# SS2D scan stage: VectorE's and GpSimd's products and scans held in the written order, and TensorE's other stages held behind the copy of dt * x

## The chip, the cores and the metric

The kernel runs on one core of a Trainium2 chip. The metric is the device time of one execution in microseconds. Engine names in profile lines: PE is TensorE's matmul, PEld its weight load, DVE is VectorE, ACT is ScalarE, POOL is GpSimd, SP is SyncE, which issues the DMAs.

## What is computed

The reference is a sequence of four vision layers on 8 images of 56 x 56 positions and 128 channels. Layers 0, 2 and 3 are deformable convolutions; layer 1 is a VMamba block (SS2D). Only layer 1 is touched. Cut to what matters:

```python
xb = silu(depthwise3x3(split(layer_norm(x) @ in_proj)) + conv_b)   # 256 channels
xs = [xb rowwise, xb columnwise, both reversed]                     # K = 4 directions
dts, B, C = split(x_proj[k] @ xs[k])                                # 8, 16 and 16 rows
dt = softplus(dt_projs[k] @ dts + bias)
h[d, n] = h[d, n] * exp(dt[d] * A[d, n]) + (dt[d] * xs[d]) * B[n]   # scan along 3136 positions
y[d] = sum over n of h[d, n] * C[n]                                 # 16 states n
out = x + out_proj(layer_norm(sum of directions + D * xs) * silu(z)); out += mlp(layer_norm(out))
```

## The kernel before

The kernel is written in a tile framework. It records instructions in the written order, but a scheduler then places them on each engine by priority and by its own model of the durations, and adds the semaphores. The order on an engine can therefore differ from the written one. `issue_after(ins)` is the way to bind it: every instruction recorded in that block on the engine of `ins` is placed after `ins`. It adds an ordering edge for the scheduler and not a wait.

Class `Vss` is layer 1. Its method `scans` runs over 128 steps (8 images, 4 directions, 4 chunks of 784 positions) and in each over 32 units. A unit is one instruction's worth of states: 32 channels (`TC`) by 4 states (`TS`) on the 128 partitions. Eight channel groups `cg` have four units `sg` = 0 to 3 each. One unit goes through these instructions (lines of the kernel before):

- `fetch_dt` and `fetch_row` (SP's DMAs) bring dt, dt * x, B and C, spread over the partitions.
- `spread`, L1297, once for each `cg`: TensorE copies dt * x into PSUM as `dtu` (one buffer of two banks, two matmuls with the identity). It is written three units ahead of unit 0 of its group, right after product 2 of the group before.
- `decay`, L1303: ScalarE writes dA = exp(dt * A) to PSUM (two buffers), one unit ahead.
- `inputs`: the product u = (dt * x) * B. For `sg` 0 to 2 VectorE makes it from `dtu` (L1313, two buffers `u`), written one unit ahead. For `sg` 3 GpSimd makes it from SBUF (L1309, one buffer `up`), written two units ahead.
- the scan, L1406: VectorE writes `h` (three buffers); its last column goes to `st` on ScalarE (L1409).
- `hc` = h * C, L1411: GpSimd (six buffers).
- `add_sums`, L1335: TensorE sums `hc` over the states into `acc`, two units at a time, written three units later. It stands already in an `issue_after` block behind the last spread.
- `open_sums` (L1327) starts `acc` (one buffer) for each 8 units, and `close_sums` (L1346) copies it out on ScalarE.

The same engines carry other work between the units. `prepare` makes the next step's rows: projections on TensorE (L1208, L1221), softplus on ScalarE, one sum and one product on GpSimd (L1228, L1230). `input_stage` is the next image's norm, the conv as nine matmuls for each tile (L1069) and the gate (L1076); `output_stage` is the norm, the output projection and the MLP of finished rows (L1130, L1152, L1170, L1181, and the transposes at L1047). They are generators that the unit loop steps: `prepare` at even units, the other two at odd units and at every fourth. All their matmuls share one PSUM buffer, `misc`, so each waits until ScalarE or VectorE has read the one before.

Of the kernel before, what the change touches and what calls it, by code (L numbers as in the profile page):

```python
# [946 lines left out]
class Vss:  # L947
# [4 lines left out]
    def __init__(self, net, images, src, dst):  # L952
        self.net, self.tc, self.nc, self.d = net, net.tc, net.nc, net.d
        self.images, self.src, self.dst = images, src, dst

    def run(self):
        tc = self.tc
        with ExitStack() as ctx:
            enter = ctx.enter_context
            self.cp = enter(tc.tile_pool(name="v_const", bufs=1))  # L960
            self.img = enter(tc.tile_pool(name="v_img", bufs=1))
            self.prep = enter(tc.tile_pool(name="v_prep", bufs=1))
            self.work = enter(tc.tile_pool(name="v_work", bufs=2))
            self.bg = enter(tc.tile_pool(name="v_bg", bufs=1))
            self.dram = enter(tc.tile_pool(name="v_dram", bufs=2, space=DRAM))
            self.pmisc = enter(tc.tile_pool(name="v_misc", bufs=1, space=PSUM))
            self.pdtu = enter(tc.tile_pool(name="v_pdtu", bufs=1, space=PSUM))
            self.pda = enter(tc.tile_pool(name="v_pda", bufs=2, space=PSUM))
            self.pacc = enter(tc.tile_pool(name="v_pacc", bufs=1, space=PSUM))
            self.weights()  # L970
            self.scans()
# [41 lines left out]

    def misc(self):
        return self.pmisc.tile([128, 512], F32, name="misc", tag="misc")

# [25 lines left out]
    def transpose(self, ps, srcs):  # L1044
        n = srcs[0].shape[0]
        for i, s in enumerate(srcs):
            self.nc.tensor.transpose(ps[:, n * i : n * (i + 1)], s, self.net.ident[:n, :n])  # L1047

    def input_stage(self, i):
        nc, w, n, T = self.nc, self.w, LC // self.NT, self.NT
        both = self.gates[i] = self.dram.tile([128, 2 * NCH, L], F32, name="gate", tag="gate")
        xn = {}

        def slab(c):
            if 0 <= c < NLC and c not in xn:
                xn[c] = self.bg.tile([128, RPC + 2, WP], F32, name="xn", tag="xn", bufs=3)
                nc.gpsimd.memset(xn[c], 0.0)
            return xn.get(c)  # L1060

        def conv(c):

            pre = self.bg.tile([128, 2 * NCH, LC], F32, name="pre", tag="pre")
            for ch in range(NCH):
                ps = self.misc()
                out = ps[:, :LC].rearrange("p (h w) -> p h w", w=W)
                for tap in range(9):
                    nc.tensor.matmul(out, lhsT=w["tap"][:, tap, 128 * ch : 128 * (ch + 1)], rhs=xn[c][:, tap // 3 : tap // 3 + RPC, tap % 3 : tap % 3 + W], start=tap == 0, stop=tap == 8)  # L1069
                    if tap % 3 == 2 and tap < 8:  # L1070
                        yield
                nc.scalar.activation(pre[:, ch, :], ps[:, :LC], AF.Identity, bias=w["conv_b"][:, ch : ch + 1])
                yield
            for ch in range(NCH):
                ps = self.misc()
                nc.tensor.matmul(ps[:, :LC].rearrange("p (h w) -> p h w", w=W), lhsT=w["in"][:, DI + 128 * ch : DI + 128 * (ch + 1)], rhs=xn[c][:, 1 : RPC + 1, 1 : W + 1], start=True, stop=True)  # L1076
                nc.scalar.copy(pre[:, NCH + ch, :], ps[:, :LC])
                yield
            last = nc.scalar.activation(pre, pre, AF.Silu)
            with self.tc.issue_after(last.ins):  # L1080
                nc.scalar.preload_act_table_set(EXP_LN)
            yield
            nc.sync.dma_start(out=both[:, :, LC * c : LC * (c + 1)], in_=pre)
            yield

        for c in range(NLC):
            xt = self.bg.tile([128, T, C], F32, name="xt", tag="xt", bufs=2)
            nc.sync.dma_start(out=xt[:n], in_=self.rows_of(self.src[i], c, n))
            yield
            yield  # L1090
            srcs = [xt[:n, t, :] for t in range(T)]
            rs = self.stats(srcs)
            yield
            z = self.bg.tile([128, T, C], F32, name="z", tag="z", padded_shape=[128, T, DI])
            self.normalize(z, srcs, rs)
            yield
            ps = self.misc()
            self.transpose(ps, [z[:n, t, :] for t in range(T)])
            rows = ps[:, :LC].rearrange("p (h w) -> p h w", w=W)
            for to, a, b, at in ((c, 0, RPC, 1), (c - 1, 0, 1, RPC + 1), (c + 1, RPC - 1, RPC, 0)):  # L1100
                s = slab(to)
                if s is not None:
                    nc.scalar.activation(s[:, at : at + b - a, 1 : W + 1], rows[:, a:b], AF.Identity, bias=w["n1b"], scale=w["n1w"])  # L1103
            yield
            if c:
                yield from conv(c - 1)
        yield from conv(NLC - 1)
# [8 lines left out]
    def output_stage(self, i, c):  # L1116
# [8 lines left out]
        for t0 in range(0, T, 2):  # L1125
            ps = self.misc()
            for t in range(2):
                at = n * (t0 + t)
                for ch in range(NCH):
                    nc.tensor.transpose(ps[:n, DI * t + 128 * ch : DI * t + 128 * (ch + 1)], y[:, ch, at : at + n], self.net.ident)  # L1130
            yield
            yield
            srcs = [ps[:n, DI * t : DI * (t + 1)] for t in range(2)]
            rs = self.stats(srcs)
            yield
            self.normalize(z[:, t0 : t0 + 2], srcs, rs)
            yield
# [11 lines left out]
        po = self.misc()  # L1149
        for t in range(T):  # L1150
            for ch in range(NCH):
                nc.tensor.matmul(po[:n, 128 * t : 128 * (t + 1)], lhsT=gT[:, ch, n * t : n * (t + 1)], rhs=w["out"][:, ch, :], start=ch == 0, stop=ch == NCH - 1)  # L1152
        yield
        yield
        nc.vector.tensor_add(xt[:n], xt[:n], po[:n].rearrange("p (t c) -> p t c", c=128))
# [11 lines left out]
        pre = self.bg.tile([128, NF, m], F32, name="pre", tag="pre", padded_shape=[128, NF, LC])  # L1167
        for f in range(NF):
            ps = self.misc()
            nc.tensor.matmul(ps[:, :m], lhsT=w["fc1"][:, 128 * f : 128 * (f + 1)], rhs=xT, start=True, stop=True)  # L1170
            nc.scalar.activation(pre[:, f, :], ps[:, :m], AF.Identity, bias=w["fc1_b"][:, f : f + 1])
            yield
        last = nc.scalar.activation(pre, pre, AF.Gelu_apprx_tanh)
# [1 line left out]
            nc.scalar.preload_act_table_set(EXP_LN)  # L1175
        yield
        po = self.misc()
        self.net.bias_row(po, n, w["fc2_b"], T)
        for t in range(T):
            for f in range(NF):  # L1180
                nc.tensor.matmul(po[:n, 128 * t : 128 * (t + 1)], lhsT=pre[:, f, n * t : n * (t + 1)], rhs=w["fc2"][:, f, :], start=False, stop=t == T - 1 and f == NF - 1)  # L1181
            if t % 2:
                yield
        nc.vector.tensor_add(xt[:n], xt[:n], po[:n].rearrange("p (t c) -> p t c", c=128))
# [13 lines left out]
    def prepare(self, s, k, c):  # L1198
# [6 lines left out]
        for b in range(2):  # L1205
            ps = self.misc()
            for ch in range(NCH):
                nc.tensor.matmul(ps[:XD, :SH].rearrange("p (a b) -> p a b", b=W), lhsT=w["xproj"][:, ch, k, :], rhs=xs[:, ch, SR // 2 * b : SR // 2 * (b + 1)], start=ch == 0, stop=ch == NCH - 1)  # L1208
            yield
            nc.scalar.copy(dbl[:, SH * b : SH * (b + 1)], ps[:XD, :SH])  # L1210
        nc.sync.dma_start(out=s["rows"].rearrange("n (x e) -> (n x) e", x=2), in_=dbl[RANK:])
# [1 line left out]
        for h in range(NCH):  # L1213
# [4 lines left out]
            for b in range(2):  # L1218
                at = slice(SH * b, SH * (b + 1))
                ps = self.misc()  # L1220
                nc.tensor.matmul(ps[:, :SH], lhsT=w["dt"][:, k, 128 * h : 128 * (h + 1)], rhs=dbl[:RANK, at], start=True, stop=True)  # L1221
                nc.scalar.activation(sp[:, at], ps[:, :SH], AF.Abs, bias=bias)
                nc.scalar.activation(dd[:, 0, at], ps[:, :SH], AF.Relu, bias=bias)
                yield
# [32 lines left out]
    def scans(self):  # L1257
# [34 lines left out]
        def spread(at, t):  # L1292
# [2 lines left out]
            ps = s["dtu", cg] = self.pdtu.tile([128, 2, 512], F32, name="dtu", tag="dtu")  # L1295
            for b in range(2):
                last = nc.tensor.matmul(ps[:, b, :SH], lhsT=self.net.ident, rhs=s["dt", cg][:, 1, SH * b : SH * (b + 1)], start=True, stop=True)  # L1297
            self.last_spread = last.ins

        def decay(at, t):  # L1300
            (i, k, c), s, (cg, sg) = steps[at], state[at], order[t]
# [3 lines left out]
        def inputs(at, t):  # L1305
            s, (cg, sg) = state[at], order[t]
            if on_pool(t):
                u = self.work.tile([128, SC], F32, name="up", tag="up", bufs=1)
                nc.gpsimd.tensor_mul(u, s["dt", cg][:, 1], s["b", sg])  # L1309
            else:  # L1310
                u = self.work.tile([128, SC], F32, name="u", tag="u", bufs=2)
                halves = [v.rearrange("p (x e) -> p x e", x=2) for v in (u, s["b", sg])]
                nc.vector.tensor_mul(halves[0], s["dtu", cg][:, :, :SH], halves[1])  # L1313
            s["u", t] = u

        def place(t):
# [11 lines left out]

        def add_sums(at, group):
            acc = state[at]["acc"]  # L1330
            with self.tc.issue_after(self.last_spread):
                for (cg, sg), hc in group:
                    for b in range(2):
                        r = 64 * b + TC * (cg % 2)
# [27 lines left out]
        for now, (at, t) in enumerate(units):  # L1362
# [40 lines left out]
            hh = self.work.tile([128, SC], F32, name="h", tag="h", bufs=3)  # L1403
            step = 1 if forward else -1
            u, dA = s.pop(("u", t)), s.pop(("dA", t))
            nc.vector.tensor_tensor_scan(hh[:, ::step], dA[:, :SC][:, ::step], u[:, ::step], st[:, t : t + 1], ALU.mult, ALU.add)  # L1406
            if c != (NSC - 1 if forward else 0):
                last = SC - 1 if forward else 0
                nc.scalar.copy(st[:, t : t + 1], hh[:, last : last + 1])  # L1409
            hc = self.work.tile([128, SC], F32, name="hc", tag="hc", bufs=6)  # L1410
            nc.gpsimd.tensor_mul(hc, hh, s["c", sg])  # L1411
            group.append((order[t], hc))
            if t % 2:
                late.append((now + 3, add_sums, (at, group)))
# [86 lines left out]
```

## Time and profile before

| | |
|---|---|
| time, median of 3 runs | 18769.62 us (18749.45 to 18785.21) |
| the profiled execution | 18768.71 us, span 18767.1 us |
| granted TensorE clock over the span | 0.804 |
| busy share of the span | PE 76%, PEld 37%, DVE 81%, ACT 60%, POOL 62% |
| the scans, first to last (L1406) | 2460.6 to 13885.8 us |
| scan, L1406 | 4096 instructions, 1837 ns (with u) and 1832 ns (with up) |
| product u, L1313 | 3072 instructions, 956 ns |
| product up, L1309 | 1024 instructions, 1860 ns |
| product hc, L1411 | 4096 instructions, 1870 ns |
| copy of dt * x, L1297 | 4096 matmul records, 643 ns |
| one tap of the conv, L1069 | 2016 matmul records, 576 ns |

A float32 matmul of the program shows as two records. In a row of instructions, the columns after the bar are busy time, mean length of one in ns, and the engine's idle time just before them with what ended it. A line of waits names who waited, for whom, the total in us, how often, and the longest one.

### The profile page before, as it was taken

The page shows a single profiled execution, that of the slowest core. Times are in us where ns is not written, and L with a number is a line of the kernel's source. Part 1 is how long each engine was busy: PE and PEld are TensorE (multiplying, and loading weights), DVE is VectorE, ACT ScalarE, POOL GpSimd, SP SyncE. Part 2 cuts the span into 40 slices and gives each one's busy share as a digit, 9 for nine tenths or more (in the row PEclk, how much of TensorE's full clock was granted, in tenths as well). Part 3 has the DMA queues.
Part 4 walks back from the last instruction along what each step waited for, and adds up shares of the span by engine and source line. Part 5 has one row for each costly group of instructions (what it writes and reads, how often), then busy time and mean ns, then how long its engine had stood idle before and what let it go on. Part 6 is the DMA issues. An engine that isn't in the chain of part 4 may idle for free. (4 is left out here: it accounts for less than half of the span.)

```text
span 18767.1 us, 237758 instructions
## 1 busy us (share of the span) xinstructions
PE 14211.3 (76%) x79747; PEld 6897.5 (37%) x79747; DVE 15283.9 (81%) x18794; ACT 11183.2 (60%) x21344; POOL 11721.8 (62%) x6462
## 2 busy tenths in 40 slices
PE   6888787678678678678778778777666888577777
PEld 4555422222222222222222222222134666455555
DVE  7777369988988988988988998899967777677776
ACT  4666555566566566566566566666554666455555
POOL 1211079988998988998998998999951121111111
PEclk6777788889889889888889888888876777677767
DMA  8888544444444444344443343444326888578777
GB/s 240 223 221 219 140 146 165 157 167 154 141 144 140 144 146 140 140 149 140 142 149 138 139 153 138 142 147 140 139 97 180 215 214 211 154 207 212 206 213 179
DMA packets 1324266, 3112.23 MB, mean 166 GB/s; under 512 B 84800, under 2 KB 876372, under 8 KB 1255196
## 3 DMA queue, kind: packets, MB, share of 16 engines
q1 hardware_dynamic: 1323020, 3096.79, 54.2%
q8 instruction: 639, 10.47, 0.2%
q14 instruction: 607, 4.97, 0.1%
HBM read 2400.54 MB, written 872.17 MB: 174 GB/s over the span
## 5 line engine op out<-in xcount | busy, mean ns | idle before, releaser
L1411 POOL TENSOR_TENSOR hc<-h,c 128x784 f32<-128x784 f32 x4096 | 7539.9, 1870 | 772.6 <-DVE h L1406 541.5
L1406 DVE TENSOR_TENSOR_SCAN h<-dA,st,u 128x784 f32<-128x784 f32 x3072 | 5567.9, 1837 | 327.3 <-ACT dA L1303 188.4
L1303 ACT ACTIVATE dA<-dt,v_A 128x784 f32<-128x784 f32 x4096 | 3743.1, 915 | 714.3 <-DVE h L1406 713.3
L1313 DVE TENSOR_TENSOR u<-dtu,b 128x784 f32<-128x784 f32 x3072 | 2871.5, 956 | 559.1 <-PE dtu L1297 554.5
L1335 PE MATMUL acc<-hc,v_sum 128*32 128x392 f32 x16384 | 3212.8, 551 | 102.8 <-POOL hc L1411 102.1
L1297 PE MATMUL dtu<-dt,ident 128*128 128x392 f32 x4096 | 2108.6, 643 | 1501.1 <-issue 1100.7
L769 PE MATMUL pt<-ident,sw 112*128 112x112 f32 (+8 forms) x11648 | 1912.5, 302 | 495.2 <-DMA sw<-skew 489.0
L736 POOL MEMSET win<- 128x1820 f32 (+2 forms) x384 | 631.5, 1648 | 2512.1 <-DMA skew<-win 1972.1
L1406 DVE TENSOR_TENSOR_SCAN h<-dA,st,up 128x784 f32<-128x784 f32 x1024 | 1876.1, 1832 | 232.1 <-POOL hc L1411 171.1
L771 ACT COPY st<-pt 128x448 f32<-128x448 f32 (+6 forms) x2912 | 1230.7, 444 | 1348.7 <-PE pt L769 1300.9
L1309 POOL TENSOR_TENSOR up<-dt,b 128x784 f32<-128x784 f32 x1024 | 1904.6, 1860 | 135.1 <-DVE h L1406 124.0
L1409 ACT COPY st<-h 128x1 f32<-128x1 f32 x3072 | 581.4, 189 | 2163.6 <-DVE h L1406 2154.8
L1297 PEld LDWEIGHTS dtu<-dt,ident 128*128 128x128 f32 x4096 | 863.4, 235 | 2555.1 <-issue 1676.0
L733 POOL TENSOR_TENSOR ay<-hat,om 112x756 f32<-112x756 f32 (+2 forms) x192 | 441.2, 2298 | 2141.6 <-ACT hat L729 1891.7
L769 PEld LDWEIGHTS pt<-ident,sw 112*128 112x128 f32 (+8 forms) x11648 | 1339.5, 171 | 1079.6 <-issue 721.0
L1335 PEld LDWEIGHTS acc<-hc,v_sum 128*32 128x32 f32 x16384 | 766.9, 117 | 2478.2 <-issue 1657.8
L745 DVE TENSOR_TENSOR win<-win,patch 112x252 f32 (+2 forms) x3456 | 1569.6, 464 | 51.6 <-DVE bn_st L847 13.7
L742 DVE TENSOR_TENSOR patch<-ay,hat 112x756 f32<-112x756 f32 (+2 forms) x1152 | 1221.9, 1074 | 437.7 <-POOL ay L733 437.4
L780 PE MATMUL yps<-st,xw 120*32 120x48 f32 (+8 forms) x23296 | 1222.2, 296 | 230.5 <-ACT st L771 184.2
L1069 PE MATMUL misc<-xn,v_tap 128*128 128x448 f32 x2016 | 871.1, 576 | 94.2 <-ACT xn L1103 60.0
L822 PE MATMUL ps<-xT,w_fc 128*128 128x448 f32 (+1 forms) x1536 | 790.9, 649 | 111.5 <-ACT xT L817 72.3
L1346 ACT COPY y<-acc 64x392 f32<-64x392 f32 x768 | 576.1, 750 | 409.8 <-PE acc L1335 401.3
(162 smaller groups left out, 19421.5 us busy)
## 6 DMA issues: line engine op xcount, KB each, us to landing
dt<-dds SPq DMA_DIRECT2D x1024, 784.0 KB
sw<-skew SPq DMA_DIRECT2D x224, 1050.0 KB
sw<-skew SPq DMA_DIRECT2D x224, 896.0 KB
b<-rows SPq DMA_DIRECT2D x512, 392.0 KB
c<-rows SPq DMA_DIRECT2D x512, 392.0 KB
dds<-dd SPq DMA_DIRECT2D x256, 784.0 KB
sw<-skew SPq DMA_DIRECT2D x224, 784.0 KB
skew<-win SPq DMA_DIRECT2D x128, 964.7 KB
```

Of the source, the lines that this page charges most:

```text
L742: nc.vector.tensor_mul(patch[:n], bcast(a, 3, KX), bcast(b, 2, KY))
L745: self.last_add = nc.vector.tensor_add(to, to, patch[:n, NCB * p : NCB * (p + 1)]).ins
L769: last = nc.tensor.transpose(ps[:KP, n * g : n * (g + 1)], sw[t0:t1, g, KP * j : KP * (j + 1)], self.net.ident[t0:t1, t0:t1])
L771: nc.scalar.copy(st[:KP, : G * n], ps[:KP, : G * n])
L780: self.nc.tensor.matmul(yps[CG * g : CG * (g + 1), t0:t1], lhsT=xw[:KP, j, CG * g : CG * (g + 1)], rhs=st[:KP, n * g : n * (g + 1)], start ...
L1297: last = nc.tensor.matmul(ps[:, b, :SH], lhsT=self.net.ident, rhs=s["dt", cg][:, 1, SH * b : SH * (b + 1)], start=True, stop=True)
L1303: nc.scalar.activation(da[:, :SC], s["dt", cg][:, 0], AF.Exp, scale=w["A"][:, k, NSG * cg + sg : NSG * cg + sg + 1])
L1309: nc.gpsimd.tensor_mul(u, s["dt", cg][:, 1], s["b", sg])
L1313: nc.vector.tensor_mul(halves[0], s["dtu", cg][:, :, :SH], halves[1])
L1335: nc.tensor.matmul(acc[r : r + TC, :SH], lhsT=w["sum"], rhs=hc[:, SH * b : SH * (b + 1)], start=False, stop=sg == NSG - 1)
L1406: nc.vector.tensor_tensor_scan(hh[:, ::step], dA[:, :SC][:, ::step], u[:, ::step], st[:, t : t + 1], ALU.mult, ALU.add)
L1411: nc.gpsimd.tensor_mul(hc, hh, s["c", sg])
```

## The change

`self.last_spread` becomes `self.last`, a dictionary with the last instruction of three kinds, and `in_line(name)` gives an `issue_after` block behind the last one of a kind (or an empty block, before there is one).

- "vector": every product u and every scan on VectorE is placed behind the one written before it.
- "pool": every product up and hc on GpSimd likewise.
- "spread": the matmuls and transposes of `prepare`, `input_stage` and `output_stage` are placed behind the last spread written before them, as the sums were already.

VectorE's norm statistics and additions, GpSimd's L1228 and L1230, ScalarE, the DMAs and `open_sums` get no edge. No arithmetic, buffer or size changes.

```diff
+    def in_line(self, name):
+        last = self.last.get(name)
+        return nullcontext() if last is None else self.tc.issue_after(last)
...
     def transpose(self, ps, srcs):
         n = srcs[0].shape[0]
         for i, s in enumerate(srcs):
-            self.nc.tensor.transpose(ps[:, n * i : n * (i + 1)], s, self.net.ident[:n, :n])
+            with self.in_line("spread"):
+                self.nc.tensor.transpose(ps[:, n * i : n * (i + 1)], s, self.net.ident[:n, :n])
...
                 for tap in range(9):
-                    nc.tensor.matmul(out, lhsT=w["tap"][...], rhs=xn[c][...], start=tap == 0, stop=tap == 8)
+                    with self.in_line("spread"):
+                        nc.tensor.matmul(out, lhsT=w["tap"][...], rhs=xn[c][...], start=tap == 0, stop=tap == 8)
...
-            self.last_spread = last.ins
+            self.last["spread"] = last.ins
...
             if on_pool(t):
-                nc.gpsimd.tensor_mul(u, s["dt", cg][:, 1], s["b", sg])
+                with self.in_line("pool"):
+                    self.last["pool"] = nc.gpsimd.tensor_mul(u, s["dt", cg][:, 1], s["b", sg]).ins
             else:
-                nc.vector.tensor_mul(halves[0], s["dtu", cg][:, :, :SH], halves[1])
+                with self.in_line("vector"):
+                    self.last["vector"] = nc.vector.tensor_mul(halves[0], s["dtu", cg][:, :, :SH], halves[1]).ins
...
-            with self.tc.issue_after(self.last_spread):
+            with self.in_line("spread"):
                 for (cg, sg), hc in group:
...
-            nc.vector.tensor_tensor_scan(hh[:, ::step], ...)
+            with self.in_line("vector"):
+                self.last["vector"] = nc.vector.tensor_tensor_scan(hh[:, ::step], ...).ins
...
-            nc.gpsimd.tensor_mul(hc, hh, s["c", sg])
+            with self.in_line("pool"):
+                self.last["pool"] = nc.gpsimd.tensor_mul(hc, hh, s["c", sg]).ins
```

The same `in_line("spread")` stands around the matmuls of L1076, L1130, L1152, L1170, L1178, L1181, L1208 and L1221.

More of the change, by code (lines that the diff above doesn't have):

```diff
@@ L954, in __init__ @@
         self.images, self.src, self.dst = images, src, dst
+        self.last = {}
     def run(self):
@@ L1068, in conv @@
                 for tap in range(9):
-                    nc.tensor.matmul(out, lhsT=w["tap"][:, tap, 128 * ch : 128 * (ch + 1)], rhs=xn[c][:, tap // 3 : tap // 3 + RPC, tap % 3 : tap % 3 + W], start=tap == 0, stop=tap == 8)
+                    with self.in_line("spread"):
+                        nc.tensor.matmul(out, lhsT=w["tap"][:, tap, 128 * ch : 128 * (ch + 1)], rhs=xn[c][:, tap // 3 : tap // 3 + RPC, tap % 3 : tap % 3 + W], start=tap == 0, stop=tap == 8)
                     if tap % 3 == 2 and tap < 8:
@@ L1075, in conv @@
                 ps = self.misc()
-                nc.tensor.matmul(ps[:, :LC].rearrange("p (h w) -> p h w", w=W), lhsT=w["in"][:, DI + 128 * ch : DI + 128 * (ch + 1)], rhs=xn[c][:, 1 : RPC + 1, 1 : W + 1], start=True, stop=True)
+                with self.in_line("spread"):
+                    nc.tensor.matmul(ps[:, :LC].rearrange("p (h w) -> p h w", w=W), lhsT=w["in"][:, DI + 128 * ch : DI + 128 * (ch + 1)], rhs=xn[c][:, 1 : RPC + 1, 1 : W + 1], start=True, stop=True)
                 nc.scalar.copy(pre[:, NCH + ch, :], ps[:, :LC])
@@ L1129, in output_stage @@
                 for ch in range(NCH):
-                    nc.tensor.transpose(ps[:n, DI * t + 128 * ch : DI * t + 128 * (ch + 1)], y[:, ch, at : at + n], self.net.ident)
+                    with self.in_line("spread"):
+                        nc.tensor.transpose(ps[:n, DI * t + 128 * ch : DI * t + 128 * (ch + 1)], y[:, ch, at : at + n], self.net.ident)
             yield
@@ L1151, in output_stage @@
             for ch in range(NCH):
-                nc.tensor.matmul(po[:n, 128 * t : 128 * (t + 1)], lhsT=gT[:, ch, n * t : n * (t + 1)], rhs=w["out"][:, ch, :], start=ch == 0, stop=ch == NCH - 1)
+                with self.in_line("spread"):
+                    nc.tensor.matmul(po[:n, 128 * t : 128 * (t + 1)], lhsT=gT[:, ch, n * t : n * (t + 1)], rhs=w["out"][:, ch, :], start=ch == 0, stop=ch == NCH - 1)
         yield
@@ L1169, in output_stage @@
             ps = self.misc()
-            nc.tensor.matmul(ps[:, :m], lhsT=w["fc1"][:, 128 * f : 128 * (f + 1)], rhs=xT, start=True, stop=True)
+            with self.in_line("spread"):
+                nc.tensor.matmul(ps[:, :m], lhsT=w["fc1"][:, 128 * f : 128 * (f + 1)], rhs=xT, start=True, stop=True)
             nc.scalar.activation(pre[:, f, :], ps[:, :m], AF.Identity, bias=w["fc1_b"][:, f : f + 1])
@@ L1177, in output_stage @@
         po = self.misc()
-        self.net.bias_row(po, n, w["fc2_b"], T)
+        with self.in_line("spread"):
+            self.net.bias_row(po, n, w["fc2_b"], T)
         for t in range(T):
             for f in range(NF):
-                nc.tensor.matmul(po[:n, 128 * t : 128 * (t + 1)], lhsT=pre[:, f, n * t : n * (t + 1)], rhs=w["fc2"][:, f, :], start=False, stop=t == T - 1 and f == NF - 1)
+                with self.in_line("spread"):
+                    nc.tensor.matmul(po[:n, 128 * t : 128 * (t + 1)], lhsT=pre[:, f, n * t : n * (t + 1)], rhs=w["fc2"][:, f, :], start=False, stop=t == T - 1 and f == NF - 1)
             if t % 2:
@@ L1207, in prepare @@
             for ch in range(NCH):
-                nc.tensor.matmul(ps[:XD, :SH].rearrange("p (a b) -> p a b", b=W), lhsT=w["xproj"][:, ch, k, :], rhs=xs[:, ch, SR // 2 * b : SR // 2 * (b + 1)], start=ch == 0, stop=ch == NCH - 1)
+                with self.in_line("spread"):
+                    nc.tensor.matmul(ps[:XD, :SH].rearrange("p (a b) -> p a b", b=W), lhsT=w["xproj"][:, ch, k, :], rhs=xs[:, ch, SR // 2 * b : SR // 2 * (b + 1)], start=ch == 0, stop=ch == NCH - 1)
             yield
@@ L1220, in prepare @@
                 ps = self.misc()
-                nc.tensor.matmul(ps[:, :SH], lhsT=w["dt"][:, k, 128 * h : 128 * (h + 1)], rhs=dbl[:RANK, at], start=True, stop=True)
+                with self.in_line("spread"):
+                    nc.tensor.matmul(ps[:, :SH], lhsT=w["dt"][:, k, 128 * h : 128 * (h + 1)], rhs=dbl[:RANK, at], start=True, stop=True)
                 nc.scalar.activation(sp[:, at], ps[:, :SH], AF.Abs, bias=bias)
@@ L1330, in add_sums @@
             acc = state[at]["acc"]
-            with self.tc.issue_after(self.last_spread):
+            with self.in_line("spread"):
                 for (cg, sg), hc in group:
@@ L1405, in scans @@
             u, dA = s.pop(("u", t)), s.pop(("dA", t))
-            nc.vector.tensor_tensor_scan(hh[:, ::step], dA[:, :SC][:, ::step], u[:, ::step], st[:, t : t + 1], ALU.mult, ALU.add)
+            with self.in_line("vector"):
+                self.last["vector"] = nc.vector.tensor_tensor_scan(hh[:, ::step], dA[:, :SC][:, ::step], u[:, ::step], st[:, t : t + 1], ALU.mult, ALU.add).ins
             if c != (NSC - 1 if forward else 0):
```

## The prediction

> **What bounds it now.** I read the busy shares first, then the busy time of each engine over the scan stage alone, then who waits there, then VectorE's timeline in a quiet stretch. The scan instructions run from 2460 to 13886 us, so layer 1's scans hold 11426 of 18767 us; the change touches nothing else. The row of that stretch (columns: length, then busy time and instructions of PE, PEld, DVE, ACT, POOL, then clock, DMA share, GB/s):
>
> ```profile
> 2460.00:13886.00 11426.00, 8633.46 (x31298) 3027.20 (x31296) 10263.40 (x8602) 7049.03 (x13027) 10430.71 (x5762) 0.86 0.42 146
> ```
>
> Two engines bound the stage together: GpSimd is idle for 995 us of it, VectorE for 1163. No change of order can take it below GpSimd's 10431. The waits of the two (total, times, longest):
>
> ```profile
> DVE u L1313 <- PE dtu L1297: 554.5, 251, 80.6
> DVE h L1406 <- ACT dA L1303: 235.7, 196, 4.2
> DVE h L1406 <- POOL hc L1411: 209.8, 164, 3.3
> ...
> DVE h L1406 <- POOL up L1309: 4.7, 5, 2.1
> ```
> ```profile
> POOL hc L1411 <- DVE h L1406: 541.5, 477, 8.4
> POOL hc L1411 <- PE acc L1335: 178.6, 116, 4.8
> POOL up L1309 <- DVE h L1406: 124.0, 52, 6.2
> ```
>
> VectorE's largest wait is for TensorE's copy of dt * x; GpSimd's is for scans that VectorE delivers late. **Exchange rates** for the sum: of about 1028 us in which VectorE waits for others than GpSimd (1243 in the idle columns of its groups, less 209.8 + 4.7), 541.5 come out as idle GpSimd, so a microsecond saved on VectorE is worth 0.53. A microsecond saved on GpSimd alone I take at 0.5: VectorE waits 214.5 us for GpSimd against some 450 us of GpSimd idle that VectorE's scans do not cause.
>
> In a quiet stretch VectorE's rows read (start, length):
>
> ```profile
> 9284.65 0.95 DVE L1313 TENSOR_TENSOR u<-dtu,b 128x784 f32<-128x784 f32 x1
> 9285.74 1.85 DVE L1406 TENSOR_TENSOR_SCAN h<-dA,st,u 128x784 f32<-128x784 f32 x1
> 9287.50 1.82 DVE L1406 TENSOR_TENSOR_SCAN h<-dA,st,up 128x784 f32<-128x784 f32 x1
> ```
>
> The first scan reads the product just before it and starts 0.14 us after that product's end; the next scan does not depend on its neighbour and starts 0.09 us before its neighbour's end.
>
> **Part 1, VectorE's order.** Call the units of one channel group 0 to 3 (3 takes its product from GpSimd). In the built order of before, product 2 stands directly ahead of its own scan in 859 of 1024 groups, product 0 comes after every scan of the group before in 760, and the rest are scattered. In the built order of after all 3072 products stand exactly one scan ahead: product 1, scan 0, product 2, scan 1, scan 2, next product 0, scan 3.
>
> (a) Adjacent dependences. Before has 612 products directly followed by the scan that reads them (trace: +133 ns against -83 ns for independent neighbours, so 0.216 us each) and 108 products that directly follow the scan whose buffer they overwrite (+34 ns, 0.117 us each): 132.2 + 12.6 = 144.8 us. After has none of the first and 851 of the second, because u has two buffers and product 2 takes the one that scan 0 just read: 851 x 0.117 = 99.6 us. Gain 45 us on VectorE, 24 us of time.
>
> The Trainium skill ("VectorE: DVE Perf Modes", section "The DRAIN you can't avoid") says a semaphore between VectorE instructions costs nothing extra: eight copies took 13.88 us with one after each or only after the last. By that this term would be zero; the rows above disagree, with 0.14 us after the end against 0.09 us before it, and the measurement decides.
>
> (b) The window for the copy of dt * x. It may start when product 2 has read the old dtu and must be done at the next product 0. Grouped by the scans that stand between these two in before, VectorE's waits at product 0 are: none, 29 groups, 73 us; one, 153 groups, 81 us; two, 765 groups, 281 us; three, 76 groups, 39 us. After has two everywhere. (The 80.6 us wait left out here is the stage's start.) Lateness is the end of the copy's last matmul plus 0.13 us, less the end of VectorE's instruction before product 0. Moving every group's lateness by 1.84 us (a scan's 1837 ns) per scan gained or lost turns 500 us into 406: 94 us on VectorE, 50 us of time.
>
> (c) The added ordering brings 657 more stand-alone semaphore instructions in VectorE's queue. I cost them at nothing: they are passed while the scan ahead runs. Without that cover, at the 50 ns median of VectorE's such rows, they cost 33 us.
>
> **Part 2, GpSimd's order.** In before, the product up stands three hc ahead of its own in 947 of 1024 groups, but five ahead in 55, where it waits for the last scan of the group before (it has one buffer) with two ready hc products queued behind it: the 124.0 us row. After has it two ahead everywhere, between hc 0 and hc 1, long after that scan. Removed: between 0 (GpSimd would have waited for VectorE anyway) and 124 us; 62 us of time at the rate above. Does the later place make scan 3 wait for up? Before, scan 3 waits for hc 0 (h has three buffers), queued behind up; after, for up, queued behind hc 0: the same 1.87 + 1.86 us of GpSimd work. I take zero; the 4.7 us row is the lower bound, the 209.8 us row twice the upper.
>
> **Part 3, TensorE's other stages behind the copy.** Each is now placed after the last written copy; what queues behind a waiting copy is the conv's nine taps, the projections and the MLP, and ScalarE waits for them. In TensorE's built order the work between the last sum ahead of a copy and that copy falls from 1374 to 1022 us over the stage (my counts by the mean length of each row), and copies with two or more such stages ahead fall from 241 to 93. But the long waits, 4 to 5 us in the conv stretches, stand where nine taps (about 7.7 us) and their neighbours are in the same places as before: spacings holding all nine are 91, from 68. Moving each lateness by its own change gives +66 us on VectorE, taking the late ones out -200; I take zero and keep both ends. The sums also wait for the copy, and the copy for product 2, which now comes one scan earlier: of GpSimd's 178.6 us wait for sums (six hc buffers), 116 times at 1.54 us, I take a third, 60 us, between 0 and all; 30 us of time.
>
> **Sum.** 24 + 50 + 62 + 30 = 166 us. The profiled execution took 18768.71 us, of which 18767.1 is the span; the median of the three runs is 18769.62, so they can stand for each other. 18768.7 - 166 = 18603; I say 18600 us.
>
> **Rivals.**
> *The copy is held by TensorE, not by product 2.* Then an earlier product 2 brings nothing, while the next product 0 stands one scan earlier and holds a ready scan 3 behind it: each of the 251 waits for dtu grows by 1.84 us, 462 us on VectorE, 245 of time; less the 166, 18850 us. For it: TensorE is 76% busy in the stage, and the last sums ahead of the copy wait for hc 1, which GpSimd now makes after up. Against: TensorE's weight loads at L1297 wait for product u 335 times, 589.9 us. It decides once more than about two thirds of the waits are of that kind (166 / 245).
> *Waits at the copy nearly vanish*, because what queued ahead was mostly movable: 554.5 x 0.53 = 294, with (a), up and sums 116, together 410: 18360 us. Against it stand the unmoved taps.
> *It shows nothing:* the order moves, VectorE's savings are taken back by GpSimd, which has 91% of the stage already: 18770 us.
>
> **Chances.** The forecast 0.50 (18500 to 18720), vanishing waits 0.12, nothing 0.14, TensorE-held 0.24. A change of under 0.2%, 37 us, can hardly be told from none; by that bound faster 0.62, same 0.14, slower 0.24. The range reaches from close to the second rival, 18390, to a little above the first, 18870; it leaves out about half of the one and a tail of the other, and covers the ends of (c) and part 3.
>
> **What would show it.** Right: the scans' stretch shortens by 100 to 250 us with busy times as they are; no product is followed at +133 ns by its scan; the row of up waiting for h goes to a few us; GpSimd's wait for acc falls under 130 us; the dtu row lies between 350 and 500 us. Wrong: a dtu row over 700 us with waits longer by a scan's length (first rival), or under 150 (second); a row of scans waiting for up of over 200 us would show GpSimd's new place mis-sized; a longer stage with shorter waits would mean that instructions themselves grew, which nothing here foresees.

## The result, and the profile after

The changed kernel is slower, by half a per cent: 18857.91 us (median of 5 runs, 18852.96 to 18875.61) against 18778.75 us for the kernel before on the same chip (5 runs, 18749.45 to 18785.21). The ratio is 1.0047, interval 1.0033 to 1.0062. The forecast was 18600 us; the time lies inside the given range of 18390 to 18870, near its upper end. The profiled execution took 18854.38 us with a span of 18852.7, 85.6 us over that of before. The stretch of the scans, 11426 us before, is 11522 us long (2447 to 13969): the whole loss and some 10 us more is in it.

The row of that stretch, in the columns of the prediction's first row (length, busy time and instructions of PE, PEld, DVE, ACT, POOL, then clock, DMA share, GB/s):

```profile
2447.00:13969.00 11522.00, 8785.91 (x31305) 3049.59 (x31303) 10296.55 (x8601) 7043.36 (x13028) 10418.91 (x5763) 0.87 0.41 145
```

GpSimd is busy for 12 us less and VectorE for 33 us more. TensorE's busy time is 152 us longer, but not its instructions: the mean of its largest group, the sums, is 547 ns (551 before), and they overlap less. The granted clock is no lower (0.87; it was 0.86). So what grew is mostly waiting. VectorE's first rows in the list of waits of the same stretch (who waited, for whom, total us, times, longest):

```profile
DVE u L1332 <- PE dtu L1314: 532.3, 241, 9.4
DVE h L1426 <- ACT dA L1320: 335.8, 202, 4.5
DVE h L1426 <- POOL up L1327: 151.5, 157, 2.2
DVE h L1426 <- POOL hc L1432: 57.9, 80, 2.9
```

Four things are to be read here. The wait for the copy of dt * x was 554.5 us with the stage's start in it (80.6) and 473.9 without; the row above has no stage start in it, so it grew by 58. The wait for ScalarE's dA rose from 235.7 to 335.8. Scans hardly waited for `up` before (4.7) and now do for 151.5 us, while their wait for `hc` fell from 209.8 to 57.9: the two together stayed where they were, 214.5 before and 209.4 after.

GpSimd's two largest rows of waits, and its two costly groups in the table by line (busy time, mean ns | idle time before them):

```profile
POOL hc L1432 <- DVE h L1426: 755.5, 696, 7.8
POOL hc L1432 <- PE acc L1354: 139.0, 76, 6.8
```
```profile
L1432 POOL TENSOR_TENSOR hc<-h,c 128x784 f32<-128x784 f32 x4096 | 7530.9, 1860 | 1021.1 <-DVE h L1426 755.5 <-PE acc L1354 139.0 <-issue 75.5
L1327 POOL TENSOR_TENSOR up<-dt,b 128x784 f32<-128x784 f32 x1024 | 1899.0, 1855 | 0.0
```

`up` itself waits for nothing now (124.0 us for scans before), as forecast. But `hc` waits 755.5 us for scans instead of 541.5: what was taken from one GpSimd instruction came back at the other, with 90 us on top.

VectorE's timeline (start, length) shows the new order at work:

```profile
8337.58 1.85 DVE L1426 TENSOR_TENSOR_SCAN h<-dA,st,u 128x784 f32<-128x784 f32 x1
8339.46 0.97 DVE L1332 TENSOR_TENSOR u<-dtu,b 128x784 f32<-128x784 f32 x1
8340.35 3.58 DVE L1426 TENSOR_TENSOR_SCAN h<-dA,st,u 128x784 f32<-128x784 f32 x2
```

Product 2 follows scan 0, whose buffer it overwrites, 0.03 us after that scan's end; the scan behind it starts 0.08 us before the product's end. No product stands directly ahead of its own scan any more.

To see which part did what, I added up VectorE's waits (those over 0.2 us) in each run's trace by cause, the stage's start left out. "GpSimd" is scans waiting for `up` or `hc`. "Gaps" is the sum of all smaller distances between neighbours; it is negative because independent neighbours overlap. Together with the lengths of its instructions, these columns make up the stretch. All in us; the experiments of the lower rows follow.

| kernel | scans' stretch | copy | dA | GpSimd | other waits | gaps |
|---|---|---|---|---|---|---|
| before | 11426 | 473 | 232 | 214 | 155 | -501 |
| after | 11522 | 531 | 335 | 209 | 114 | -549 |
| VectorE's edges alone | 11423 | 611 | 258 | 110 | 122 | -536 |
| GpSimd's edges alone | 11548 | 491 | 240 | 329 | 128 | -486 |
| the same, up one unit earlier | 11470 | 471 | 243 | 243 | 157 | -512 |
| TensorE's edges alone | 11652 | 612 | 310 | 199 | 157 | -476 |
| VectorE's and GpSimd's | 11519 | 613 | 310 | 158 | 110 | -531 |
| VectorE's and TensorE's | 11425 | 555 | 317 | 141 | 92 | -548 |
| all, up one unit earlier | 11432 | 555 | 339 | 135 | 79 | -544 |
| all, product 0 behind scan 3 | 11502 | 236 | 478 | 349 | 104 | -536 |
| all, both of these | 11357 | 279 | 469 | 184 | 97 | -552 |
| VectorE's and TensorE's, product 0 behind scan 3 | 11358 | 278 | 458 | 184 | 112 | -554 |

Before to after: copy +58, dA +103, GpSimd -5, others -41, gaps -48, and 29 us more of instruction lengths (10852 to 10881): together the stretch's +95. The lengths are no finding: with GpSimd's edges alone and `up` one unit earlier, where VectorE's order is almost that of before, they are 10868.

### The profile page after: what moved, and what is told of

Same layout as the page of the kernel before. It is cut to its first block, busy times and chain, and to the rows that moved or that the text cites. A ratio compares the mean times of both kernels' runs of the same rounds, so it can differ in the third digit from the quotient of the medians.

```text
span 18852.7 us, 238449 instructions
## 1 busy us (share of the span) xinstructions
PE 14366.8 (76%) x79747; PEld 6922.9 (37%) x79747; DVE 15305.7 (81%) x18794; ACT 11178.5 (59%) x21344; POOL 11709.7 (62%) x6462
## 5 line engine op out<-in xcount | busy, mean ns | idle before, releaser
L1432 POOL TENSOR_TENSOR hc<-h,c 128x784 f32<-128x784 f32 x4096 | 7530.9, 1860 | 1021.1 <-DVE h L1426 755.5
L1354 PE MATMUL acc<-hc,v_sum 128*32 128x392 f32 x16384 | 3404.7, 547 | 358.9 <-POOL hc L1432 358.0
L1332 DVE TENSOR_TENSOR u<-dtu,b 128x784 f32<-128x784 f32 x3072 | 2948.0, 960 | 641.7 <-PE dtu L1314 612.1
L780 PEld LDWEIGHTS yps<-st,xw 120*32 120x32 f32 (+2 forms) x23296 | 542.1, 126 | 709.9 <-ACT st L771 252.5
```

What stands on the lines that cost most here:

```text
L780: self.nc.tensor.matmul(yps[CG * g : CG * (g + 1), t0:t1], lhsT=xw[:KP, j, CG * g : CG * (g + 1)], rhs=st[:KP, n * g : n * (g + 1)], start ...
L1332: self.last["vector"] = nc.vector.tensor_mul(halves[0], s["dtu", cg][:, :, :SH], halves[1]).ins
L1354: nc.tensor.matmul(acc[r : r + TC, :SH], lhsT=w["sum"], rhs=hc[:, SH * b : SH * (b + 1)], start=False, stop=sg == NSG - 1)
L1432: self.last["pool"] = nc.gpsimd.tensor_mul(hc, hh, s["c", sg]).ins
```

## The experiments

All ratios are to the kernel before on the same chip, with a 95% interval. The experiments ran on three chips, whose medians for the kernel before are 18756, 18756 and 18771 us, so what an edit is worth is taken from the ratios and not from the times.

### Each set of edges alone

The first three keep the edges of one engine. `in_line` is cut to one name; the sums keep the block behind the last spread that they had before the change.

```diff
-        last = self.last.get(name)
+        last = self.last.get(name) if name in ("vector",) else None    # ("pool",), ("spread",)
...
-            with self.in_line("spread"):
+            with self.tc.issue_after(self.last["spread"]):             # in add_sums
```

**VectorE's edges alone.**

> VectorE's edges alone: products u and scans in the written order, GpSimd and TensorE's other stages as before. Theory V (the loss comes with VectorE's order, which in the built order also brings the second projection of the MLP between the two matmuls of a copy of dt * x, 168 matmuls as in the full change): ratio to before 1.003 to 1.007, waits for the copy 530 to 620 us, scans' wait for dA over 300 us. Theory T (the loss comes with TensorE's edges): the adjacent dependences pay, 45 to 60 us faster, ratio 0.996 to 0.998, dA waits about 236 us.

Measured: 18767.12 us, 1.0005 (0.9996 to 1.0014): no difference, which neither theory expected. VectorE's rows of waits:

```profile
DVE u L1332 <- PE dtu L1314: 612.6, 302, 7.7
DVE h L1426 <- ACT dA L1320: 260.1, 184, 4.0
DVE h L1426 <- POOL hc L1432: 101.7, 103, 2.6
```

The gaps shrink by 35 us and GpSimd's rows halve (214 to 110 us), and the copy's row takes it back: 611 instead of 473. With VectorE bound, the scheduler by itself put `up` three units ahead in 1004 of 1024 groups.

**GpSimd's edges alone.**

> GpSimd's edges alone: up two products ahead in all 1024 groups, none five ahead. Forecast's part 2: the 124 us wait of up goes and 62 us of time with it, ratio 0.996 to 0.998. Rival (what the full change's trace suggests, where GpSimd's wait for scans grew by as much): the wait goes and the time stays, 0.999 to 1.001, with the scans' wait for GpSimd moved from hc to up at the same total, about 210 us.

Measured: 18858.61 us, 1.0051 (1.0037 to 1.0065): as slow as the whole change, and outside both forecasts.

```profile
DVE u L1332 <- PE dtu L1314: 492.2, 242, 8.8
DVE h L1426 <- POOL up L1327: 278.7, 202, 4.4
DVE h L1426 <- ACT dA L1320: 243.6, 203, 4.7
DVE h L1426 <- POOL hc L1432: 51.1, 52, 4.1
```

Copy and dA are nearly as before; the new row is that of scans waiting for `up`. The wait for GpSimd did not keep its total of some 210 us, it grew to 329.

**TensorE's edges alone.**

> TensorE's edges alone: the other stages behind the last written copy, VectorE and GpSimd free. Theory T: ratio 1.004 to 1.008, waits for the copy over 600 us. Theory V: 0.998 to 1.002. Its built order has 67 products up five ahead (before 55) and 674 products directly ahead of their own scan (before 612), which cost some 13 us more on VectorE under both.

Measured: 18980.92 us, 1.0117 (1.0101 to 1.0132): the slowest of all, beyond theory T's range.

```profile
DVE u L1332 <- PE dtu L1314: 613.6, 309, 9.2
DVE h L1426 <- ACT dA L1320: 314.6, 217, 6.7
```

The edges meant for the copy lengthen its wait by 139 us here. In the built order VectorE's free order had become less even as well: 674 products directly ahead of their own scan (612 before), and 67 `up` five units ahead (55 before). Why the scheduler answers so was not followed further.

### Pairs of edges

```diff
+        last = self.last.get(name) if name in ("vector", "pool") else None     # TensorE's left out
+        last = self.last.get(name) if name != "pool" else None                 # GpSimd's left out
```

The first line is one kernel and the second another; in the first the sums keep their block, as above.

> VectorE's and GpSimd's edges, without TensorE's new ones. Theory V: like the full change, ratio 1.003 to 1.007. Theory T: 0.993 to 0.998, the sum of the two parts alone.

Measured: 18829.59 us, 1.0039 (1.0026 to 1.0053).

> VectorE's and TensorE's edges without GpSimd's; up falls three ahead in 1005 groups and never five. Theory G: as the run with up early, within 0.15% of it, ratio 0.996 to 1.001, because it is the place of up and not the binding that costs. If the binding itself cost something, this run is faster than that one. Rival V: 1.003 to 1.006.

Measured: 18750.12 us, 0.9995 (0.9986 to 1.0004).

So with VectorE's edges in place TensorE's do cut the copy's wait (611 to 555), and no net time comes of it: dA takes 59 us more. The first of the two runs lies in theory V's range, but VectorE's edges alone had cost nothing; the second lies in theory G's. The loss comes with GpSimd's edges, both with and without TensorE's (1.0005 to 1.0039, and 0.9995 to 1.0047). TensorE's edges lose as well when they stand alone, but not on top of VectorE's.

### Is it the binding of GpSimd, or the place that it binds `up` to?

The change leaves `up` where it is written: two units ahead of its scan, which on GpSimd is between `hc` 0 and `hc` 1 of its group. Writing it one unit earlier puts it ahead of `hc` 0, three units ahead, with every edge of the change kept.

```diff
-            if now + 2 < len(units) and on_pool(units[now + 2][1]):
-                inputs(*units[now + 2])
+            if now + 3 < len(units) and on_pool(units[now + 3][1]):
+                inputs(*units[now + 3])
```

> The full change with one edit: the product up is written three units ahead and so stands ahead of hc 0 again (three ahead in all 1024 groups), still bound to the written order. VectorE's and TensorE's built orders have the same counts as the full change's. Theory G (GpSimd's new place for up is the loss: its margin before scan 3 fell from 3.3 to 0.8 us, so that the preparation of dt and dt * x on GpSimd now ends in VectorE's time): the scans' wait for up falls from 151 to under 20 us, their wait for all of GpSimd from 209 to about 110, ratio to before 0.997 to 1.001, so some 70 to 130 us faster than the full change. Rival V (VectorE's fixed order costs it, whatever GpSimd does): 1.003 to 1.006 as the full change.

Measured: 18763.43 us, 1.0002 (0.9993 to 1.0011): the whole loss is gone. Nearly the whole order of the other engines is that of the change: in the two traces TensorE's differs in 8 of 79747 places and VectorE's in 26 of 18794. The stretch's row and VectorE's waits (the first of them has the stage's start in it, 81.3):

```profile
2435.00:13868.00 11433.00, 8778.27 (x31307) 3041.84 (x31307) 10288.83 (x8602) 7042.49 (x13028) 10422.90 (x5764) 0.87 0.41 146
```
```profile
DVE u L1332 <- PE dtu L1314: 636.9, 246, 81.3
DVE h L1426 <- ACT dA L1320: 339.2, 201, 4.5
DVE h L1426 <- POOL hc L1432: 133.9, 157, 2.7
```

Against the change the stretch is 90 us shorter. VectorE's waits for GpSimd fall by 74 us (209.4 to 135.0) and its other waits by 35; the copy's wait rises by 24, and dA stays high. And it equals the kernel without GpSimd's edges (0.9995 and 1.0002, intervals overlap): behind VectorE's and TensorE's edges the binding costs nothing that shows, its place does.

How the place costs is less plain than the row of `up` suggests, and the timeline shows why. First GpSimd after the change, and the scan that waits:

```profile
8472.87 1.86 POOL L1432 TENSOR_TENSOR hc<-h,c 128x784 f32<-128x784 f32 x1 [1.37 <-DVE h L1426]
8474.69 1.84 POOL L1245 TENSOR_TENSOR dd<-dd,sp 128x784 f32<-128x784 f32 x1
8476.61 2.23 POOL L1247 TENSOR_TENSOR dd<-dd,xb 128x784 f32<-128x784 f32 x1
8478.81 1.89 POOL L1432 TENSOR_TENSOR hc<-h,c 128x784 f32<-128x784 f32 x1
8480.64 1.87 POOL L1327 TENSOR_TENSOR up<-dt,b 128x784 f32<-128x784 f32 x1
```
```profile
8482.54 1.85 DVE L1426 TENSOR_TENSOR_SCAN h<-dA,st,up 128x784 f32<-128x784 f32 x1 [1.82 <-POOL up L1327]
```

`dd`, the next step's sum and product (4.07 us), stands in the queue, and `hc` 0 and `up` come behind it; scan 3 needs both. The same group with `up` one unit earlier:

```profile
8412.18 1.86 POOL L1432 TENSOR_TENSOR hc<-h,c 128x784 f32<-128x784 f32 x1 [1.36 <-DVE h L1426]
8414.00 1.84 POOL L1245 TENSOR_TENSOR dd<-dd,sp 128x784 f32<-128x784 f32 x1
8415.80 1.84 POOL L1327 TENSOR_TENSOR up<-dt,b 128x784 f32<-128x784 f32 x1
8417.60 2.26 POOL L1247 TENSOR_TENSOR dd<-dd,xb 128x784 f32<-128x784 f32 x1
8419.83 5.49 POOL L1432 TENSOR_TENSOR hc<-h,c 128x784 f32<-128x784 f32 x3
```
```profile
8421.74 1.85 DVE L1426 TENSOR_TENSOR_SCAN h<-dA,st,up 128x784 f32<-128x784 f32 x1 [1.71 <-POOL hc L1432]
```

At this group the wait only changes its name, 1.82 to 1.71 us: where GpSimd is behind, the two orders are the same work. The difference is made where GpSimd is ahead. With `up` two units ahead it stands idle in front of `hc` 0 until scan 0 ends, and does `up` after that: counted over the trace, 368 us of idle time in front of `hc` 0, against 1 us with `up` earlier, when `up` fills that time. Most of this only moves: in front of `hc` 1 to 3 GpSimd is idle for 653 us after the change and for 909 with `up` earlier. The row of `hc` with `up` earlier, to be read against the 1021.1 us above, leaves 111 us net:

```profile
L1432 POOL TENSOR_TENSOR hc<-h,c 128x784 f32<-128x784 f32 x4096 | 7526.5, 1862 | 910.0 <-DVE h L1426 635.1 <-PE acc L1354 131.5 <-issue 64.4
```

With `up` behind `hc` 0, `hc` 1 ends later behind its scan (lower quartile 2.84 against 2.03 us, median 2.89 against 2.60), and 189 of the 256 `dd` pairs stand directly behind `hc` 1 or `hc` 2, so they begin later too. Scan 3's waits for GpSimd fall from 148.9 us (155) to 106.5 (111), and scan 2's from 45.2 to 17.6. From `up`'s end to scan 3's start the median is 1.49 us after the change and 4.13 us with `up` earlier (lower quartiles 0.76 and 3.23); after the change, `dd` stood in the 12 us ahead of `up`'s end at 134 of the 154 waits of scan 3 for `up`, and at 291 of all 1024 groups. The 90 us are shown by the run; this path inside them is read from the two traces.

The same move with GpSimd's edges alone:

```diff
+        last = self.last.get(name) if name in ("pool",) else None     # the sums keep their block, as above
...
+            if now + 3 < len(units) and on_pool(units[now + 3][1]):
+                inputs(*units[now + 3])
```

> GpSimd's edges alone with up written three units ahead: VectorE's and TensorE's built orders have the counts of the kernel before, and on GpSimd only the 77 groups change in which up stood two, four or five ahead. What the prediction's 62 us for the blocks of up is worth by itself: by the prediction ratio 0.996 to 0.998; by the rival (GpSimd then waits for VectorE's scans instead) 0.999 to 1.001 with the wait of up gone and its wait for scans grown by about as much.

Measured: 18799.81 us, 1.0015 (1.0006 to 1.0024), against 1.0051 with `up` two ahead: the place is worth 0.36% here, some 68 us. GpSimd's rows of waits:

```profile
POOL hc L1432 <- DVE h L1426: 518.6, 466, 8.4
POOL hc L1432 <- PE acc L1354: 271.7, 132, 10.0
```

This kernel is also the cleanest test of the prediction's 62 us. It is the kernel before with its scattered `up` products put back to three ahead: in the trace TensorE's order is that of before, VectorE's differs in 24 places and GpSimd's in 193. Instead of a gain it is 0.15% slower. `up` no longer waits (124.0 us before), but `hc` waits 93 us longer for TensorE's sums (178.6 before), while its wait for scans hardly moves (541.5 before). GpSimd's idle time in front of `up` and `hc` together is 923 us, against 908 before. Taking the blocks of `up` out is worth nothing here.

### Is the copy held by TensorE or by product 2?

Product 0 of the next group stands one scan ahead of scan 3 after the change. Here it is made behind scan 3, which gives the copy three scans instead of two.

```diff
-                if not on_pool(units[now + 1][1]):
+                if not on_pool(units[now + 1][1]) and sg < NSG - 1:
                     inputs(*units[now + 1])
...                                                          # right after the scan
+            if sg == NSG - 1 and now + 1 < len(units):
+                inputs(*units[now + 1])
```

> The full change with one edit: product 0 is written behind scan 3 of the group before it, so that three scans stand between product 2 and product 0 instead of two. Theory C (the copy of dt * x is held by TensorE's other work and not by product 2, and product 0 ahead of scan 3 makes every such wait longer): waits for the copy fall from 531 us to 200 to 300, by up to 1.84 us for each of 235, ratio to the full change 0.985 to 0.993, to before 0.990 to 0.998. Rival (the copy follows product 2, so that its wait moves with the window's start): waits for the copy stay at 450 us or more and the ratio to before at 1.003 to 1.006.

Measured: 18836.06 us, 1.0040 (1.0027 to 1.0054).

```profile
DVE h L1426 <- ACT dA L1320: 478.6, 263, 7.2
DVE h L1426 <- POOL up L1327: 329.3, 219, 3.6
DVE u L1332 <- PE dtu L1314: 236.2, 131, 9.0
DVE h L1426 <- ACT st L1431: 54.5, 41, 7.0
```

The copy's wait falls by 295 us, into theory C's range, so the window does set it. This alone does not tell the two theories apart, since a third scan gives time to a copy that follows product 2 as well. The traces do: after the change no wait is left behind an unbroken copy that started as soon as product 2 was done (below). But theory C's ratio was missed, and the time hardly moves. Scan 3 now comes a product (0.95 us) earlier, with `up` still two ahead: its wait for `up` doubles, and the median distance from `up`'s end to scan 3 falls from 1.49 to 0.62 us. Scan 3's dA too has a product's time less: one scan, 1.84 us, instead of 2.79. The rows of GpSimd (+139) and dA (+142) ate what the longer window saved.

Then both together: `up` three ahead and product 0 behind scan 3, with all edges of the change; and the second without GpSimd's edges.

```diff
+            if now + 3 < len(units) and on_pool(units[now + 3][1]):        # first kernel only
+                inputs(*units[now + 3])
...
+        last = self.last.get(name) if name != "pool" else None             # second kernel only
...
+                if not on_pool(units[now + 1][1]) and sg < NSG - 1:         # both
...
+            if sg == NSG - 1 and now + 1 < len(units):                      # both
+                inputs(*units[now + 1])
```

> The full change with both edits: up written three units ahead and product 0 behind scan 3. Theory G and C together: with product 0 behind scan 3 alone the wait for the copy fell by 295 us but scan 3, now 0.95 us earlier, waited 177 us more for up and the scans 142 us more for dA; with up early its wait goes (329 to under 20 us) and part of it comes back at hc (20 to 120-160 us). Ratio to before 0.992 to 0.997. Rival (the wait for dA takes up what up gives back): 0.998 to 1.002, dA over 550 us.

Measured: 18699.72 us (18685.34 to 18711.31), 0.9962 (0.9949 to 0.9976).

> The same without GpSimd's edges (VectorE's and TensorE's alone, product 0 behind scan 3): up falls three ahead in 949 groups, five ahead in 34. If five ahead costs as its wait of 2.4 us each suggests, 0 to 0.2% slower than the run with GpSimd bound; otherwise equal to it. Ratio to before 0.992 to 0.998.

Measured: 18695.79 us, 0.9963 (0.9949 to 0.9977).

Both beat the kernel before and the changed one, within the forecast ratios, and they are equal: the 34 groups with `up` five ahead cost nothing that shows. The stretch's row and the waits of the first:

```profile
2452.00:13810.00 11358.00, 8715.09 (x31307) 3043.26 (x31307) 10288.80 (x8601) 7047.98 (x13028) 10466.24 (x5764) 0.86 0.41 147
```
```profile
DVE h L1426 <- ACT dA L1320: 470.1, 261, 8.4
DVE u L1332 <- PE dtu L1314: 279.2, 127, 9.0
DVE h L1426 <- POOL hc L1434: 185.6, 157, 2.7
DVE h L1426 <- ACT st L1431: 56.9, 47, 7.0
```

With the place of `up` out of the way, the longer window is worth 0.40%, some 75 us, and the stretch is 75 us shorter. Of the 276 us by which the copy's wait falls, 130 come back as waits for dA, 49 as waits for `hc` and 50 as waits for st. dA is now the largest wait.

## Why the prediction was wrong, step by step

**Part 2, the place of `up`, is the step that failed.** It turned the result into a loss; without it the time is that of before (1.0002), and the forecast's 166 us are still missing, for which the steps below answer. Part 2 argued that scan 3 waits for the same 1.87 + 1.86 us of GpSimd work whichever comes first, and took zero. The amount of work is the same, but not when it may begin: `up` is free once scan 3 of the group before has ended, `hc` 0 only when scan 0 has. Put first, `up` fills GpSimd's idle time; put second, it adds to what follows. By the ratios the place costs some 68 us with GpSimd's edges alone (1.0051 less 1.0015) and some 85 in the full change (1.0047 less 1.0002). The mark that was set for it, a row of `up` over 200 us, was not reached (151.5), since most of that row is the old wait for `hc` under another name; GpSimd's two rows had to be read as a sum, against the 110, 135 and 141 us that they have where `up` stands earlier, VectorE is bound and product 0 is in its place.

**Part 2, the 62 us for the blocks** did not come either. `up`'s 124.0 us went to zero as forecast, but the run that does only this shows no gain: GpSimd then waits at `hc`, for TensorE's sums. The rate of 0.5 for a microsecond saved on GpSimd was taken from two totals and from no row that shows such a saving arrive; it was zero.

**Part 1 (b), the window of the copy,** had the wrong sign: 406 us forecast, 531 measured. It matters whether other matmuls stand between the two halves of a copy. Whole copies cost VectorE 362 us of waiting before and 318 after; split ones, which are no more in number (116 and 111), 111 and 215. What product 2 held did vanish: the waits behind whole copies that started as soon as product 2 was done went from 65.4 us (54) to none. The waits behind whole copies that TensorE started late hardly grew, from 297 to 317 us. So the growth of 58 us is in the split copies. In group 14 of seven of the eight images the MLP's second projection now stands in such a copy, and VectorE waits 4.9 to 9.4 us there (0.15 us at most before), 44 us in all. The shift by 1.84 us per scan took each copy's end as given, while TensorE's own order changed with VectorE's.

The first rival named the right engine, TensorE, at eight times the price (462 us against 58), and its sum is off in its own terms: it lets an earlier product 2 bring nothing and yet takes off the whole 166 us, which hold 50 for just that. With 116 it would have been 18900 us. That the measured time is near its 18850 is chance.

TensorE's sums, which stand ahead of copies, also wait longer for `hc`: the idle time before their matmuls, before and after the change. How much of the copy's wait comes of that was not measured.

```profile
L1335 PE MATMUL acc<-hc,v_sum 128*32 128x392 f32 x16384 | 3212.8, 551 | 102.8 <-POOL hc L1411 102.1
L1354 PE MATMUL acc<-hc,v_sum 128*32 128x392 f32 x16384 | 3404.7, 547 | 358.9 <-POOL hc L1432 358.0
```

**Part 3** was taken as zero for the copy, between +66 and -200. On top of VectorE's edges it is -56 (611 to 555) to -82 (613 to 531), inside these ends, with no net time. Alone the edges cost 1.2%, which no end of the sum allowed for. The sums' part came two thirds right: GpSimd's wait for acc fell by 40 us, from 178.6 to 139.0, where 60 were taken; no run shows time won by it.

**dA was not in the sum.** Its wait grew by 103 us, the largest single term of VectorE's account. VectorE's edges alone bring 25, GpSimd's 8, TensorE's 77; VectorE's with GpSimd's bring 78 and with TensorE's 84. With `up` earlier it stays at 339 us and the time is that of before, so it did not make the loss, but it is part of why no gain came. What on ScalarE comes late, and whether the place of dA could be moved, was not tried, and stays open.

**The exchange rates** took VectorE's savings at about half. (The 0.53 counts the 80.6 us at the stage's start among the waits, which no order inside the stage can save; without them it is 0.57.) VectorE's waits, gaps and lengths add up to the stretch by their definition, so a wait removed counts fully when no other takes its place, and nothing when one does. No fixed rate came out of the runs: 295 us off the copy's wait were worth 20 us of the stretch with `up` two ahead, and 276 us were worth 75 with `up` three ahead.

**What held:** (a) 45 us on VectorE forecast, 48 measured in the gaps (-501 to -549). The trace after has no product at +133 ns from its own scan, 851 scans followed at +34 ns by the product that overwrites their buffer, and -84 ns at the other neighbours. The statement in the Trainium skill that the prediction weighed ("VectorE: DVE Perf Modes", section "The DRAIN you can't avoid") would have made this term zero. These distances show a second time that it doesn't carry over to an instruction that waits for its neighbour: the page's copies measure a semaphore after each, and here the measurement decides. (c) shows no cost in the gaps, and the busy times of VectorE and GpSimd stayed within 0.4%. The stretch was forecast 100 to 250 us shorter and is 95 longer.

## What to carry to other kernels

When an order is fixed on an in-order engine, ask of each instruction not only how long the work ahead of it is, but when each piece is free to start: put the piece with the oldest inputs first, where it fills idle time. Read the waits of one engine for another as a sum, because a wait that changes its name looks like a loss in one row and a gain in another. And forecast what is late next by its own row (here dA and `hc` behind the copy) before a saving is counted: 276 us taken from the largest wait were worth 75.

## What the runs showed of the hardware

Nothing unexpected of the chip itself. The distances between VectorE's neighbours (128 x 784, f32) were the same before and after: about +133 ns when a scan reads the product directly ahead, +34 ns when a product overwrites what the scan ahead has read, and -83 to -84 ns when the two are independent.
